# First attention of a four-layer network: norming two of eight batches ahead and six inside its loop, weighing a unit later, turning output rows in the sums' bank, first key copy on ACT

## The chip, the cores and the metric

One core of a Trainium2 chip runs the whole network in one launch. The metric is the time of that launch on the device, in microseconds; smaller is better. The engines are PE (matrix products; PEld is its loading of the stationary operand), DVE (vector), ACT (scalar functions), POOL and SP, whose queue issues most of the transfers. Each runs its own instructions in order and waits for the others on semaphores.

## The reference, cut to what matters

Four layers, each a norm, an attention and a feed-forward block that gates it. Only the first layer's norm and attention, and weights prepared for later layers, are touched. For x of 8 batches of 512 tokens with 128 features:

```python
x = L0_attn_x
xn = _layernorm(x, axis=-1)
s = _L0_attn_ref(xn, Wq, bq, Wk, bk, Wv, bv, Wo, bo)
g = _silu(_L0_ffn_ref(xn, ...))
x = x + s * g
...
def _layernorm(x, axis=-1, eps=1e-05):
    m = jnp.mean(x, axis=axis, keepdims=True)
    v = jnp.var(x, axis=axis, keepdims=True)
    return (x - m) / jnp.sqrt(v + eps)
...
# _sliding_window_attn: 16 heads of 8, blocks of 64 queries, each over its own and the previous block of keys
scores = jnp.einsum('bhnqd,bhnkd->bhnqk', qb, kw) * scale
valid = (t <= s_ + W) & (t >= s_ + 1) & (n * W - W + t >= 0)
scores = jnp.where(valid, scores, NEG)
attn = jax.nn.softmax(scores, axis=-1)
out = jnp.einsum('bhnqk,bhnkd->bhnqd', attn, vw)
out = out.transpose(...).reshape(B, S, D)
return out @ Wo.T + bo
```

## The kernel before

Tokens stand in the free dimension (x and xn are 128 features by 4096 tokens), in eight batches of 512. `network` loads x in eight pieces, loads constants of later layers, norms all eight batches (`layer_norm`), decodes the feed-forward block's weights (`l0_decode`), fills constants of layers 3 and 2 (`l2.fill`, `l1.fill`), runs `l0_attention`, then `l0_ffn`, and prepares scalars of the fourth layer (`l3_scalars`).

A framework places the semaphores and the buffers: a tile is written when the earlier tile in its buffer has been read by all its readers. What is issued through `in_order` keeps the written order on its engine; what isn't (`l0_decode`, `l3_scalars`, POOL's fills) is moved to where the framework finds room. So in the trace `l3_scalars` and the mixing weights of `l1.fill` run between 30 and 42 us, ahead of the attention's first scores.

`layer_norm` works on 512 tokens at a time: `centre` multiplies by a centring matrix into a PSUM bank (ps_c, tokens now in partitions), `spread` squares on ACT, sums on DVE (var) and takes the power -1/2 on POOL (rstd), `scale` multiplies on DVE (row), `turn` transposes back on PE (ps_t), `keep` copies to xn on ACT.

`l0_attention` first projects batch 0 (`project`: keys ps_k, copied four times under four head masks to kb, by DVE for c = 0 and 2 and by ACT for c = 1 and 3; queries ps_q; values ps_v in two parts of 4 and 3 windows). Then it runs a loop over 64 units, eight for each batch. Unit u is 128 queries and 8 heads:

- `scores(u)`: four products into a two-bank tile sc, DVE scales and masks it to e (the first DVE group called e), DVE takes the maximum mx, POOL subtracts it
- the exponential on ACT
- `turned(u)`: eight transposes on PE to two banks tp, ACT copies to pt
- `weigh(u)`: 64 by 9 products of pt with the values and a column of ones, into the bank of sums (av)
- after each pair of units, `norm`: DVE's reciprocal rec and product o; `out_rows`: PE turns o (tpo), ACT adds a bias into ot
- after each batch, `finish`: the output projection ps_o, which DVE scales to s

In iteration u each engine gets, in this order: turn of unit u, norm of the pair that ended with u-1 (u even), scores of u+3, output rows of that pair, exponential of u+2, weighing of u, `finish` of the batch before at the second unit of a batch, one step of the next batch's projection (ps_k in the first unit, the other two key copies in the second, ps_q, ps_v, ps_v). From unit 33 on a step of the feed-forward block's low-rank weights (`l0_low_rank`) comes once in eight units.

PSUM has eight banks: four for sc, three (pool p_t) for tp, tpo, ps_k, ps_q, ps_v and ps_o in turn, and one for av:

```python
sums = p_av.tile([P, 2, H, HD + 1], F32, tag="av", name="av")
...
tp = p_t.tile([P, 4, P], F32, tag="t", name="tpo")
pe.transpose(tp[:, 0, :], o.rearrange("p h d -> p (h d)"), net.ident)
```

All instructions issued through `in_order` carry one line, 84, in the profile; groups are told apart by the names of their tiles.

Of the kernel before, what the change touches and what calls it, by code (L numbers as in the profile page):

```python
# [9 lines left out]
F32 = mybir.dt.float32  # L10
I32 = mybir.dt.int32
AF = mybir.ActivationFunctionType
ALU = mybir.AluOpType
# [4 lines left out]
B = 8  # L18
# [9 lines left out]
class Net:  # L28
# [120 lines left out]

    def layer_norm(self, x, xn, gamma=None, beta=None, banks=(5, 3), free=False):  # L150

# [6 lines left out]
        with tc.tile_pool(name="ln_s", bufs=3) as sp, tc.tile_pool(  # L158
# [40 lines left out]

            for t in range(NTB + 3):  # L200
                if t < NTB:
                    centre(t)
                    spread(t)
                if 2 <= t < NTB + 2:
                    scale(t - 2)
                if t >= 3:
                    turn(t - 3)
                    keep(t - 3)
# [48 lines left out]

def l0_attention(net, xn, s_out, p0, w, bias):

# [5 lines left out]
    with ExitStack() as st:  # L265
# [22 lines left out]

        sums = p_av.tile([P, 2, H, HD + 1], F32, tag="av", name="av")

# [5 lines left out]
        def project(b):  # L296
# [5 lines left out]
            kb[b] = p2.tile([P, 4, S], F32, tag="kb", name="kb")  # L302
            for c in range(4):
                hm, hb = net.hm4[:, c : c + 1], kbias[:, c : c + 1]
                if c % 2:
                    act.activation(kb[b][:, c, :], ps, AF.Identity, scale=hm, bias=hb)
                    yield
                else:
                    dve.tensor_scalar(kb[b][:, c, :], ps, hm, hb, ALU.mult, ALU.add)
            ps = p_t.tile([P, S], F32, tag="t", name="ps_q")  # L310
            pe.matmul(ps, lhsT=w[:, 0, :], rhs=xb, start=True, stop=True)
# [46 lines left out]
        def turned(u):  # L358

            pts = []  # L360
            for g in range(2):
                tp = p_t.tile([P, 4, P], F32, tag="t", name="tp")
                for j in range(4):
                    pe.transpose(tp[:, j, :], e[u][:, 4 * g + j, :], net.ident)
                pt = p3.tile([P, 4, P], F32, tag="pt", name="pt")
                act.copy(pt, tp)
                pts.append(pt)
            return pts
# [25 lines left out]
        def out_rows(u, o):  # L394
            b, m = u // U, u // 2 % 4
            tp = p_t.tile([P, 4, P], F32, tag="t", name="tpo")
            pe.transpose(tp[:, 0, :], o.rearrange("p h d -> p (h d)"), net.ident)
            if m == 0:
                ot[b] = p2.tile([P, S], F32, tag="ot", name="ot")

            act.activation(ot[b][:, ts(m, P)], tp[:, 0, :], AF.Identity, bias=bias[:, 2:3])

# [10 lines left out]
        act.activation(e[0], e[0], AF.Exp)  # L413
        act.activation(e[1], e[1], AF.Exp)
        todo = iter(())
        for u in range(N + 2):
            if u < N and u % U == 0 and u // U + 1 < B:
                todo = project(u // U + 1)
            ended = u >= 1 and u <= N and u % 2 == 0
            if u < N:  # L420
                pts = turned(u)
            if ended:
                o = norm(u - 1)
            if u + AHEAD < N:
                scores(u + AHEAD)
            if ended:
                out_rows(u - 1, o)
            if u + 2 < N:
                act.activation(e[u + 2], e[u + 2], AF.Exp)
            if u < N:  # L430
                weigh(u, pts)
            if u >= U and u % U == 1:
                finish(u // U - 1)
            next(todo, None)
            if u == 4 * U:
                low = net.prep.l0_low_rank(
                    p0, lambda name: p_t.tile([P, S], F32, tag="t", name=name), pe, dve, act
                )
            if u > 4 * U and u % U == 6:
                next(low, None)  # L440


# [289 lines left out]
class L1Consts:  # L732
    E = 8

    def __init__(self, net, st):
        nc, tc, E = net.nc, net.tc, self.E
        self.net = net
        self.p1 = p1 = st.enter_context(tc.tile_pool(name="a1_c", bufs=1))
        self.rw = net.load(p1, "m1_r")
# [6 lines left out]
    def fill(self):  # L746
        net, nc, p1, E = self.net, self.net.nc, self.p1, self.E
        act = net.in_order(nc.scalar)
        self.w13 = net.load(p1, "m1_w13", act)
        self.w2 = net.load(p1, "m1_w2", act)  # L750

        w, par = self.w, self.par
        self.td = td = p1.tile([P, 1], F32, tag="td", name="td")
        act.activation(td, par[:, 0:1], AF.Exp)
        act.activation(td, td, AF.Copy, scale=-1.0)
        self.tf = par[:, 1:2]
        self.wm = wm = p1.tile([P, 3, 2, P], F32, tag="wm", name="wm")
        self.rest = rest = p1.tile([P, 3], F32, tag="rest", name="rest")
        act.activation(rest, par[:, 2:5], AF.Identity, scale=-1.0, bias=net.ones[:, 0:1])
        for i in range(3):  # L760
            act.activation(wm[:, i, 0, :], w[:, i, :], AF.Copy, scale=par[:, 2 + i : 3 + i])
            act.activation(wm[:, i, 1, :], w[:, i, :], AF.Copy, scale=rest[:, i : i + 1])
        act.activation(w[:, 3, :], w[:, 3, :], AF.Copy, scale=0.5)

# [20 lines left out]
        nc.gpsimd.memset(self.keep, 1.0)  # L785
        nc.gpsimd.memset(self.keep[:, :, 0:1], 0.0)


# [553 lines left out]
class L2Consts:  # L1342
# [4 lines left out]
    def __init__(self, net, st):  # L1347
# [4 lines left out]
        self.net = net  # L1352
        self.p1 = p1 = st.enter_context(tc.tile_pool(name="a2_c", bufs=1))
        self.w = net.load(p1, "a2_w")
# [1441 lines left out]
class Prepared:  # L2796
# [28 lines left out]

    def l0_decode(self):
        nc, wt, qw, sc = self.net.nc, self.f0_wt, self.qw, self.sc
        nc.vector.tensor_copy(wt, qw)
        nc.vector.tensor_scalar(wt, wt, 1.0 / 7.5, -1.0, ALU.mult, ALU.add)
        nc.vector.tensor_tensor(wt, wt, sc, ALU.mult)  # L2830

# [32 lines left out]

    def l3_scalars(self):

# [7 lines left out]
        raw = par[:, 1:5, :]  # L2874
        nc.vector.scalar_tensor_tensor(sp, raw, -1.0, raw, ALU.mult, ALU.min)
        nc.scalar.activation(sp, sp, AF.Exp)
        nc.scalar.activation(sp, sp, AF.Ln, bias=net.ones[:, 0:1])
        nc.vector.scalar_tensor_tensor(sp, raw, 0.0, sp, ALU.max, ALU.add)
        sig2, eta2, gam2, nu = (sp[:, i, :] for i in range(4))

        def vec(tag):
            return p1.tile([P, H], F32, tag=tag, name=tag)

        mu, nmu, v_e2, v_0, coef = vec("mu"), vec("nmu"), vec("v_e2"), vec("v_0"), vec("coef")
        nc.scalar.activation(mu, par[:, 0, :], AF.Exp, scale=-1.0)
        nc.vector.tensor_scalar(mu, mu, 1.0, None, ALU.add)
        nc.vector.reciprocal(mu, mu)
        nc.vector.tensor_scalar(mu, mu, 1e-4, None, ALU.add)
        nc.vector.tensor_scalar(nmu, mu, -1.0, None, ALU.mult)

        nc.vector.tensor_scalar(v_e2, nmu, 2.0, None, ALU.mult)
        nc.vector.reciprocal(v_e2, v_e2)
        nc.vector.tensor_tensor(v_e2, v_e2, sig2, ALU.mult)
        nc.vector.tensor_tensor(v_0, eta2, gam2, ALU.add)
        nc.vector.tensor_tensor(v_0, v_0, v_e2, ALU.subtract)
        nc.vector.tensor_scalar(coef, nu, float(DH), -0.5, ALU.add, ALU.mult)
        nc.vector.tensor_tensor(coef, coef, par[:, 5, :], ALU.mult)


        norm_0 = vec("norm_0")  # L2900
        nc.vector.tensor_tensor(norm_0[0:64], nu[0:64], v_e2[0:64], ALU.mult)
        nc.vector.tensor_tensor(norm_0[64:128], nu[64:128], v_0[64:128], ALU.mult)
        cs, ncs, inv_cs, g_v = vec("cs"), vec("ncs"), vec("inv_cs"), vec("g_v")


        nc.vector.scalar_tensor_tensor(cs, coef, -1.0, coef, ALU.mult, ALU.max)
        nc.vector.tensor_scalar(cs, cs, 1e-18, 2e-18, ALU.is_lt, ALU.mult)
        nc.vector.tensor_tensor(cs, cs, coef, ALU.add)
        nc.vector.tensor_scalar(ncs, cs, -1.0, None, ALU.mult)
        nc.vector.reciprocal(inv_cs, cs)  # L2910
        nc.vector.tensor_scalar(g_v, coef, -1.0, -0.5 * DH, ALU.mult, ALU.add)
        nc.vector.tensor_tensor(g_v, g_v, inv_cs, ALU.mult)
        self.scalars = nu, nmu, v_e2, v_0, norm_0, ncs, inv_cs, g_v


def network(tc, ins, out):
    with ExitStack() as ctx:
# [12 lines left out]
        with tc.tile_pool(name="prep_0", bufs=1) as p0:  # L2930
            w0, b0 = net.load(p0, "a0_w"), net.load(p0, "a0_b")
            prep.l0_load(p0)
            net.layer_norm(x, xn)
            prep.l0_decode()
            l2.fill()
            l1.fill()
            l0_attention(net, xn, s, p0, w0, b0)
            l0_ffn(net, x, xn, s, l1)
        prep.l3_scalars()
        l1_layer(net, x, xn, s, l1, l2)  # L2940
# [84 lines left out]
```

## Time and profile before

| what | us |
|---|---|
| median of 9 runs (lowest to highest) | 2330.58 (2326.09 to 2338.16) |
| the profiled execution | 2335.12 |
| its span | 2333.4 |
| busy over the span: PE, DVE, ACT, POOL | 2187.9, 2004.1, 1848.4, 1573.2 |
| busy from 100 to 150: PE, DVE, ACT, POOL | 47.81, 35.63, 33.16, 22.90 |
| first norm's first and last copy to xn | 13.40 and 29.11 |
| first scores of the attention | 42.44 |
| first turn tp (unit 0) | 50.12 |
| first product of the feed-forward block | 324.30 |

Durations of single instructions in the loop, by the rows of the trace from 100 to 315 us: e 1.22 and mx 1.22 on DVE, the subtraction 1.90 on POOL, the exponential 1.06 and a pt copy 0.59 on ACT, ot 0.37, rec 0.25, o 0.29, a key copy 0.81 on DVE and 0.78 on ACT. A view of the timeline has start, duration, engine, line, operation, output and inputs with shapes, the count, and in brackets how long the engine was idle before it and who released it. PE's listed durations overlap, since its matmuls are pipelined; the distance between starts is the cost of one.

### The profile page before, as it was taken

How to read it: one execution, taken by the hardware profiler on the slowest of the kernel's cores; microseconds unless marked ns; L12 is line 12 of the kernel's file. 1: busy time of each engine (PE TensorE's matmuls, PEld its weight loads, DVE VectorE, ACT ScalarE, POOL GpSimd, SP SyncE). 2: the span in 40 equal slices, each digit the busy share in tenths (PEclk: the TensorE clock that was granted, in tenths of full speed). 3: DMA queues.
4: the chain of work that ended last, by engine and by line, in shares of the span. 5: the costliest groups of instructions: out<-in, count | busy, mean ns of one | idle time of the engine just before them, and what ended most of it. 6: DMA issues, size and time to landing. Idle time of an engine off the chain costs nothing.

```text
span 2333.4 us, 48928 instructions
## 1 busy us (share of the span) xinstructions
PE 2187.9 (94%) x17762; PEld 1529.4 (66%) x17762; DVE 2004.1 (86%) x3595; ACT 1848.4 (79%) x3882; POOL 1573.2 (67%) x1410
## 2 busy tenths in 40 slices
PE   6999997999987999868999999999999999999998
PEld 4666675746633666645777777777777776777796
DVE  4677769786686999759999999999999999999885
ACT  4566656555543899838999999999999999999974
POOL 5344445264275788757788888888888888888644
PEclk7799989899997999979999999999999999999998
DMA  4000000012210000234443444444444444333200
GB/s 144 2 2 2 2 1 19 19 51 70 48 49 19 3 17 16 66 91 107 106 106 94 106 110 105 105 102 105 108 101 103 111 105 104 100 98 101 54 1 37
DMA packets 91617, 156.94 MB, mean 67 GB/s; under 512 B 20144, under 2 KB 44464, under 8 KB 91120
## 3 DMA queue, kind: packets, MB, share of 16 engines
q1 hardware_dynamic: 86736, 140.95, 23.1%
q0 software_dynamic: 4352, 8.92, 1.5%
q10 hardware_dynamic: 288, 3.93, 0.4%
q8 instruction: 142, 2.33, 0.4%
q14 instruction: 99, 0.81, 0.1%
HBM read 30.52 MB, written 12.06 MB: 18 GB/s over the span
## 4 chain that ended last, share of the span: by engine, by line
PE 58%; DVE 28%; POOL 5%; issue 3%; ACT 3%; DMA 2%; SPq 1%; DVEq 0%; ACTq 0%; POOLq 0%
PE sc L84 11%; DVE sc L84 7%; PE ps_av L84 6%; DVE r L84 6%; DVE y L84 6%; PE tp L84 5%; PE ps_u L84 5%; PE ps_kq L84 5%; PE av L84 3%; PE ps_n L84 3%; PE ps_ab L84 3%; PE ps_v L84 2%; DVE mx L84 2%; DVE e L84 2%; PE ps_y L84 1%
## 5 line engine op out<-in xcount | busy, mean ns | idle before, releaser
L84 POOL TENSOR_TENSOR ek<-E,kn 128x512 f32<-128x512 f32 (+3 forms) x512 | 434.1, 870 | 203.1 <-DMA kn<-nr 189.5
L84 POOL TENSOR_TENSOR e<-e,mx 128x1024 f32<-128x1024 f32 x112 | 212.1, 1900 | 190.3 <-DVE mx L84 93.5
L84 PE MATMUL sc<-r 128*128 128x512 f32 (+3 forms) x1024 | 306.6, 442 | 25.9 <-DVE y L84 18.9
L84 POOL TENSOR_TENSOR r<-r,rs 128x1024 f32<-128x1024 f32 x128 | 304.0, 2375 | 21.4 <-DMA rs<-r 18.6
L84 PE MATMUL ps_av<-u,at 128*128 128x128 f32 x2560 | 306.8, 275 | 0.3 <-DVE at L84 0.3
L84 PEld LDWEIGHTS ps_av<-u,at 128*128 128x128 f32 x2560 | 296.1, 192 | 1.5 <-ACT at L84 0.8
L84 ACT ACTIVATE y<-y,mn 128x384 f32<-128x384 f32 (+3 forms) x512 | 288.8, 570 | 4.0 <-DVE mn L84 3.2
L84 PEld LDWEIGHTS sc<-r 128*128 128x128 f32 x1024 | 164.1, 190 | 188.7 <-issue 115.4
L84 DVE CUSTOM_DVE_ANT_0 y<-y,ps_g,ncs 128x256 f32<-128x256 f32 (+3 forms) x512 | 254.0, 542 | 0.8 <-ACT y L84 0.8
L84 DVE SCALAR_TENSOR_TENSOR y<-sc,qn,V 128x512 f32<-128x512 f32 (+3 forms) x512 | 246.8, 544 | 8.6
L84 ACT ACT_TABLE_LOAD x179 | 229.7, 1283 | 6.1 <-DVE ex L84 2.1
L84 PEld LDWEIGHTS tp<-ident,y 128*128 128x128 f32 x1280 | 160.4, 140 | 112.1 <-issue 48.0
L84 PE MATMUL tp<-ident,y 128*128 128x128 f32 x1280 | 201.8, 273 | 2.6 <-ACT o L84 2.0
L84 DVE TENSOR_TENSOR sc<-sc,EF 128x1280 f32<-128x1280 f32 x128 | 191.9, 1499 | 4.3
L84 ACT COPY at<-tp 128x512 f32<-128x512 f32 x376 | 191.3, 509 | 5.2 <-PE tp L84 1.5
L84 DVE SCALAR_TENSOR_TENSOR sc<-sc,ek 128x1280 f32<-128x1280 f32 x128 | 189.9, 1483 | 2.9 <-POOL ek L84 1.4
L84 ACT ACTIVATE y<-y 128x1280 f32<-128x1280 f32 x128 | 163.4, 1277 | 6.0 <-DVE y L84 5.3
L84 DVE TENSOR_TENSOR r<-sn,ps_kq 128x1024 f32<-128x1024 f32 x128 | 155.4, 1214 | 12.1 <-ACT sq L84 12.1
L84 ACT ACTIVATE sq<-ps_kq 128x1024 f32<-128x1024 f32 x128 | 131.7, 1029 | 34.0 <-PE ps_kq L84 34.0
L84 DVE TENSOR_TENSOR r<-ct,ps_kq 128x1024 f32<-128x1024 f32 x128 | 155.4, 1214 | 0.0
L84 POOL TENSOR_TENSOR s<-s,o 128x512 f32<-128x512 f32 x116 | 148.4, 1279 | 2.5 <-ACT o L84 2.4
L84 ACT ACTIVATE e<-e 128x1024 f32<-128x1024 f32 x112 | 117.3, 1061 | 40.4 <-POOL e L84 39.9
(462 smaller groups left out, 5042.1 us busy)
## 6 DMA issues: line engine op xcount, KB each, us to landing
rs<-r SPq DMA_DIRECT2D x256, 256.0 KB, 3.8
kn<-nr SPq DMA_DIRECT2D x512, 64.0 KB, 2.0
yrows<-yy SPq DMA_DIRECT2D x36, 128.0 KB, 1.8
ct<-trig SPq DMA_DIRECT2D x16, 256.0 KB
EF<-E SPq DMA_DIRECT2D x16, 256.0 KB, 2.7
EF<-E SPq DMA_DIRECT2D x16, 192.0 KB
m_w<-m_w ACTq DMA_DIRECT2D x1, 2560.0 KB, 9.3
x<-x SPq DMA_DIRECT2D x8, 256.0 KB, 3.7
```

What stands on the lines that cost most here:

```text
L84: ins = op(*args, **kwargs)
```

## The change

- `layer_norm` takes a count and norms two batches ahead. The other six are normed inside the attention's loop: centring (four products on PE, a copy to SBUF on ACT), square (ACT), sums (DVE) and root (POOL), scaling (four ACT instructions in place of one on DVE), turn and copy, each at a given unit.
- `weigh` of a unit is issued one iteration later, so the pair's norm and output rows come at odd units and `finish` at the third unit of a batch. pt has four buffers instead of three.
- The output rows are turned into the free columns of the bank that holds the sums (av), not into a bank of p_t.
- ACT makes the first key copy (c = 1), then DVE (c = 0), then ACT, then DVE.
- Loads of later layers' constants come behind the first layer's loads on SP's queue; the two large expert weights go from ACT's queue to SP's. `l0_decode` (its last product on POOL instead of DVE), the mixing weights of `l1.fill` and `l3_scalars` become steps that are issued in order in the loop, three to a batch from unit 9 on.

```diff
-    def layer_norm(self, x, xn, gamma=None, beta=None, banks=(5, 3), free=False):
+    def layer_norm(self, x, xn, gamma=None, beta=None, banks=(5, 3), free=False, n=NTB):
...
-            for t in range(NTB + 3):
-                if t < NTB:
+            for t in range(n + 3):
+                if t < n:
...
-        sums = p_av.tile([P, 2, H, HD + 1], F32, tag="av", name="av")
+        both = p_av.tile([P, TB], F32, tag="av", name="av")
+        n_av = 2 * H * (HD + 1)
+        sums = both[:, 0:n_av].rearrange("p (m h d) -> p m h d", m=2, h=H)
+        tpo = both[:, n_av : n_av + P]
...
-            for c in range(4):
+            for c in (1, 0, 3, 2):
                 hm, hb = net.hm4[:, c : c + 1], kbias[:, c : c + 1]
                 if c % 2:
                     act.activation(kb[b][:, c, :], ps, AF.Identity, scale=hm, bias=hb)
-                    yield
                 else:
                     dve.tensor_scalar(kb[b][:, c, :], ps, hm, hb, ALU.mult, ALU.add)
+                    yield
...
-                pt = p3.tile([P, 4, P], F32, tag="pt", name="pt")
+                pt = p5.tile([P, 4, P], F32, tag="pt", name="pt")
...
-            tp = p_t.tile([P, 4, P], F32, tag="t", name="tpo")
-            pe.transpose(tp[:, 0, :], o.rearrange("p h d -> p (h d)"), net.ident)
+            pe.transpose(tpo, o.rearrange("p h d -> p (h d)"), net.ident)
...
-            act.activation(ot[b][:, ts(m, P)], tp[:, 0, :], AF.Identity, bias=bias[:, 2:3])
+            act.activation(ot[b][:, ts(m, P)], tpo, AF.Identity, bias=bias[:, 2:3])
...
+        def centre(b):
+            ps = p_t.tile([P, 4, P], F32, tag="t", name="ps_c")
+            for k in range(4):
+                pe.matmul(
+                    ps[:, k, :], lhsT=x[:, ts(4 * b + k, P)], rhs=net.cmat,
+                    start=True, stop=True,
+                )
+            mid[b] = p2.tile([P, 4, P], F32, tag="lc", name="lc")
+            act.copy(mid[b], ps)
+
+        def square(b):
+            sqs[b] = p2.tile([P, 4, P], F32, tag="sq", name="sq")
+            act.activation(sqs[b], mid[b], AF.Square, scale=net.inv_root)
+
+        def spread(b):
...
+            dve.tensor_reduce(var, sqs.pop(b), AX.X, ALU.add)
+            dve.tensor_scalar(var, var, EPS, None, ALU.add)
+            pool.tensor_tensor(std[b], var, net.neg_half.to_broadcast([P, 4]), ALU.pow)
+
+        def scale_rows(b):
+            for k in range(4):
+                act.activation(
+                    mid[b][:, k, :], mid[b][:, k, :], AF.Copy, scale=std[b][:, k : k + 1]
+                )
+
+        def turn_rows(b):
+            ps = p_t.tile([P, 4, P], F32, tag="t", name="ps_t")
+            for k in range(4):
+                pe.transpose(ps[:, k, :], mid[b][:, k, :], net.ident)
+            act.copy(xn[:, ts(b, S)], ps.rearrange("p k q -> p (k q)"))
+
+        norms = {}
+        for b in range(2, B):
+            c = U * (b - 3) + 7 if b > 2 else 1
+            for part, at in (
+                (centre, c), (square, c + 1), (spread, c + 2), (scale_rows, c + 4),
+                (turn_rows, U * (b - 2) + 6),
+            ):
+                norms.setdefault(at, []).append((part, b))
+
+        def early():
+            yield from net.prep.l0_decode(dve, pool)
+            yield from l1.mixing(act)
+            yield from net.prep.l3_scalars(dve, act)
+
+        rest = early()
         todo = iter(())
-        for u in range(N + 2):
+        pts = {}
+        for u in range(N + 3):
             if u < N and u % U == 0 and u // U + 1 < B:
                 todo = project(u // U + 1)
-            ended = u >= 1 and u <= N and u % 2 == 0
+            ended = u >= 3 and u % 2 == 1
             if u < N:
-                pts = turned(u)
+                pts[u] = turned(u)
             if ended:
-                o = norm(u - 1)
+                o = norm(u - 2)
             if u + AHEAD < N:
                 scores(u + AHEAD)
             if ended:
-                out_rows(u - 1, o)
+                out_rows(u - 2, o)
             if u + 2 < N:
                 act.activation(e[u + 2], e[u + 2], AF.Exp)
-            if u < N:
-                weigh(u, pts)
-            if u >= U and u % U == 1:
+            if 1 <= u <= N:
+                weigh(u - 1, pts.pop(u - 1))
+            if u >= U and u % U == 2:
                 finish(u // U - 1)
             next(todo, None)
+            for part, b in norms.get(u, ()):
+                part(b)
+            if u >= U and u % U in (1, 3, 6):
+                next(rest, None)
...
-            if u > 4 * U and u % U == 6:
+            if u > 4 * U and u % U == 5:
                 next(low, None)
...
     def fill(self):
...
-        self.w13 = net.load(p1, "m1_w13", act)
-        self.w2 = net.load(p1, "m1_w2", act)
+        self.w13 = net.load(p1, "m1_w13")
+        self.w2 = net.load(p1, "m1_w2")
...
+    def mixing(self, act):
...
+        for i in range(3):
+            act.activation(wm[:, i, 0, :], w[:, i, :], AF.Copy, scale=par[:, 2 + i : 3 + i])
+            act.activation(wm[:, i, 1, :], w[:, i, :], AF.Copy, scale=rest[:, i : i + 1])
+            yield
...
-        nc.vector.tensor_tensor(wt, wt, sc, ALU.mult)
+        pool.tensor_tensor(wt, wt, sc, ALU.mult)
+        yield
...
+        dve.scalar_tensor_tensor(sp, raw, -1.0, raw, ALU.mult, ALU.min)
+        act.activation(sp, sp, AF.Exp)
+        act.activation(mu, par[:, 0, :], AF.Exp, scale=-1.0)
+        yield
+        act.activation(sp, sp, AF.Ln, bias=net.ones[:, 0:1])
+        yield
...
             prep.l0_load(p0)
-            net.layer_norm(x, xn)
-            prep.l0_decode()
+            l2.load()
+            l1.load()
+            net.layer_norm(x, xn, n=2)
             l2.fill()
             l1.fill()
-            l0_attention(net, xn, s, p0, w0, b0)
+            l0_attention(net, x, xn, s, p0, w0, b0, l1)
             l0_ffn(net, x, xn, s, l1)
-        prep.l3_scalars()
```

## The prediction

> **What bounds the kernel now.** I read the busy time by stretch first, then the timeline of the head (0 to 62 us), then TensorE's own timeline through the loop, then the rows of single tiles. The change touches only what runs before 324 us, where the first feed-forward block begins; nothing behind it is edited, and the scalars for the fourth layer that move into the loop are needed only much later.
>
> The stretches (busy time of each engine, then granted clock, DMA share, GB/s):
>
> ```profile
> 0.00:20.00 20.00, 11.45 (x59) 11.10 (x60) 7.58 (x17) 6.04 (x9) 13.84 (x59) 0.91 0.70 212
> 20.00:60.00 40.00, 26.82 (x144) 17.22 (x146) 21.44 (x47) 18.82 (x36) 15.82 (x19) 0.63 0.27 104
> 60.00:100.00 40.00, 39.52 (x414) 25.54 (x406) 22.89 (x26) 20.34 (x32) 14.48 (x8) 0.73 0.01 2
> 100.00:150.00 50.00, 47.81 (x636) 31.20 (x628) 35.63 (x42) 33.16 (x54) 22.90 (x13) 1.00 0.01 2
> ```
>
> From 100 us on PE is busy 47.8 of 50, DVE 35.6, ACT 33.2, POOL 22.9: the loop is PE's. Before 60 us no engine is full: that is a chain. And the clock is 0.63 and 0.73 of full until about 82 us, with PE busy all the while.
>
> The head, from the timeline (start, duration, then what):
>
> ```profile
> 10.88 4.00 POOL L84 TENSOR_TENSOR rstd<-var,neg_half 128x4 f32<-128x4 f32 x4
> 11.96 0.69 DVE L84 TENSOR_TENSOR row<-ps_c,rstd 128x512 f32<-128x512 f32 x1 [0.82 <-POOL rstd L84]
> 13.40 0.59 ACT L84 COPY xn<-ps_t 128x512 f32<-128x512 f32 x1 [2.00 <-PE ps_t L84]
> ...
> 29.75 2.07 PE L84 MATMUL ps_k<-xn,a_w 128*128 128x512 f32 x2 [0.68 <-ACT xn L84]
> 36.19 0.76 ACT L84 ACTIVATE kb<-ps_k,kbias,hm 128x512 f32<-128x512 f32 x1
> 36.97 1.28 ACT L2877 ACT_TABLE_LOAD   x1
> 40.05 0.76 ACT L84 ACTIVATE kb<-ps_k,kbias,hm 128x512 f32<-128x512 f32 x1
> 40.86 1.65 PE L84 MATMUL ps_v<-a_w,xn 128*128 128x128 f32 x6 [6.18 <-ACT kb L84]
> 42.44 1.95 PE L84 MATMUL sc<-kb,q 32*64 32x512 f32 x16
> ```
>
> Eight batches are normed until 29.7; then ACT makes its first key copy at 36.2 and its second at 40.05, with the other layers' preparation ahead of them, and the first scores start at 42.44.
>
> The loop at full clock:
>
> ```profile
> 128.03 0.30 PE L84 MATMUL tpo<-ident,o 128*128 128x128 f32 x1 [0.24 <-DVE o L84]
> 128.26 1.11 PE L84 MATMUL av<-vw,pt 128*64 128x9 f32 x32
> 128.37 0.37 ACT L84 ACTIVATE ot<-tpo,a_b 128x128 f32<-128x128 f32 x1 [0.47 <-PE tpo L84]
> 130.46 0.81 DVE L84 TENSOR_SCALAR kb<-ps_k,hm,kbias 128x512 f32<-128x512 f32 x1
> 131.30 0.78 ACT L84 ACTIVATE kb<-ps_k,kbias,hm 128x512 f32<-128x512 f32 x1 [0.76 <-DVE kb L84]
> 132.61 1.13 PE L84 MATMUL av<-vw,pt 128*64 128x9 f32 x32 [0.30 <-ACT pt L84]
> 134.63 0.60 PE L84 MATMUL tp<-ident,e 128*128 128x128 f32 x4
> 135.71 0.66 PE L84 MATMUL tp<-ident,e 128*128 128x128 f32 x4 [0.48 <-DVE s L84]
> ```
>
> One batch of eight units (first turn of one batch, 130.25, to that of the next, 162.10) takes 31.85 us. PE's holes in it: 0.31 twice where the output rows' turn waits for DVE's o (the last sc ends at 127.72, tpo starts at 128.03), 0.37 where av waits for pt, 0.57 where the second tp waits for a bank that DVE's s still reads, 0.14 behind one more tpo: 1.7 in all. The work itself is 30.1.
>
> **The change, part by part.** The sum is made against the profiled execution, 2335.1 us (its span is 2333.4, and 1.7 lie around it); the median shown is 2330.6.
>
> Head. Two batches are normed instead of eight. POOL's root still comes at 10.88 (it is behind the same fills); the second root ends at 12.9, its rows are scaled (0.69), turned (0.7 to 0.8) and copied (0.59), so ps_k can start at about 15.1 instead of 29.75: 14.6 saved. The attention's weights, issued at 12.2 us on SP's queue now, go right behind x there (4.5 us), so they aren't late. Then the chain without the strangers: ps_k 2.07, four key copies one after the other (0.2 to start, 0.78 and 0.81 alternating), the second ps_v (1.55), then scores: 7.0 us against 12.7 (29.75 to 42.44). Saved: 5.7. Head **-20.3** (from -18, if the fills or masks are later, to -24, if POOL's roots come when var is ready at 7.9). The two large expert weights go from ACT's queue to SP's: the timeline has 1.10 us for these two issues on ACT, inside the 5.7; on SP they stand behind everything needed early.
>
> Norms woven in. Per batch PE gets eight instructions of ps_c (0.128 each as ps_v, 8 in 1.00) and four turns (0.51): 1.54, for six batches **+9.2**. ACT gets a copy 0.59, square 0.60, four row scalings of about 0.3 (the 128x128 copies at 34.2 have that step), a copy 0.59: 3.0 per batch, onto 21.7 of 31.85. DVE gets 0.9, POOL one root of 1.0. All three stay under PE, so they are costed at nothing, except that behind the last turn (unit 7 of 8) ACT comes to the output rows late by about 0.25: +1.5.
>
> Weighing a unit later takes the 0.37 pt wait away; turns and centring between units give DVE time for o, which takes the 0.31s away; no tpo in the three banks takes the 0.57 and the 0.14 mostly away. Removed: 1.7 in each of six warm batches, some 2 in the others: **-12.3**. Given back: the turn of unit 3 finds its second bank held by s or q for about 0.3, seven times: +2.1.
>
> Output rows in the sums' bank. This is the dearest edit. Two engines never read one bank together in this trace: 14 times ACT's key copy waits for DVE's key copy of the same ps_k, though neither needs the other's data (131.30 above, straight after 130.46+0.81):
>
> ```profile
>   DVE kb L84: 26.3, 14
> ```
>
> So I take it that PE's av, which now writes the bank that ACT's ot reads, waits for ot too. In the rows above av starts 0.23 behind tpo; ot ends at 128.74, and PE's starts follow ACT's ends by 0.06 (322.38 to 322.44), so av would start at 128.80: 0.54 later. Thirty-two such units: **+17.3**. Nothing else is on PE's queue ahead of the stalled av that could fill it; scores, turns and projections stand behind. Lower bound 0 (if regions of a bank are told apart), upper 0.9 (ACT one ot late).
>
> [...]
>
> First key copy by ACT. DVE's first copy now waits for ACT's. ps_k ends, 0.2, ACT 0.78, DVE 0.72 to its successor, and the successor is now rec of an ended unit (odd units end now): rec 0.28, o 0.29, 0.12 to tpo: 2.42 after ps_k, where PE, with tp 0.97 and sc 1.02, is there at 1.99. 0.44, seven times: **+3.1** (0 to 5).
>
> Preparation moved into the loop: some 35 small DVE and ACT instructions of 0.1 to 0.55 us, and POOL's 128x768 product (1.4 by its 128x1024 row of 1.90), hidden under PE, whose cover is a unit's slack in pt. Ln's table and Exp's again (1.28 each) meet one unit: **+2** (0 to 4).
>
> Clock. In this execution it stayed at half from 50 to 81.8 us, which cost some 15; it fell for 3.4 us at 170.5 and 269.5, each behind the stretch with split tp, sc, tpo and av, and from 310 to 327. The batch behind the start now has centring beside the projections, so I expect it up a unit or two earlier: -6 (0 to -10). But holes of 0.5 to 1.0 beside sc and av make more such thin stretches: +6 (0 to +15). Net **0**.
>
> [...]
>
> Sum: -20.3 +9.2 +1.5 -12.3 +2.1 +17.3 +3.1 +2 +0 = +2.6: **2337.7**, said as 2338, which is 0.3% over the median of 2330.6. About 0.2% (4.7 us) is what can be told from no change.
>
> **The rivals.**
>
> The bank doesn't stall PE (faster). If av starts 0.23 behind tpo as now, 17.3 go: 2320. For it: the columns are disjoint, and a write beside a read of the same bank isn't shown in this trace. Against it: the 14 waits. It decides from a stall under 0.16 us, where the sum passes 2325.9.
>
> The clock gains (about no change). Everything as forecast, but the start is up 10 earlier and no new falls come: 2338-10 = 2328. For it: six centrings and turns are full-size matmuls. Against: the holes.
>
> The clock falls in most batches (slower). Two falls a batch of 3.4 us at half rate, plus one that lasts until the next projections, 15 us over the loop: 2353. For it: a hole of 0.98 in the first ended unit of a batch stands between sc and av, longer than the 0.57 behind which it fell twice. Against: it didn't fall behind the 0.31s.
>
> **How the numbers follow.** Forecast 0.45 (its own range 2327 to 2349); no bank stall 0.25; clock gains 0.12; clock falls 0.18. Low end: 2320 less 4 for a longer head gain, 2316. High end: 2353 and 3 more for ACT's lateness, 2356. Faster by over 0.2%: 0.25, half of 0.12, and 0.03 of the forecast, 0.34. Slower: 0.18 and 0.30 of the forecast, 0.48. Within: 0.18.
>
> **What would show it.** First scores near 22 us, not 42. Per ended unit: av starts right behind ot's end (0.06), not 0.23 behind tpo. A warm batch of 34.5 us, not 31.85. DVE's key copy waits for ACT's, and tpo behind it waits for o. The feed-forward block starts near 327, not 324. Wrong: av not waiting for ot; a head that gains under 15; a clock at half much longer or shorter than 30 us.

## The result, and the profile after

The changed kernel takes 2385.91 us (median of 15 runs, 2362.69 to 2396.98) beside 2329.24 (46 runs of the kernel before): **ratio 1.0243, 95% interval 1.0227 to 1.026**. It is 2.4% slower; 2338 was forecast, and 2356 was the range's upper end. The profiled execution took 2381.53 us, with a span of 2379.8.

The stretches of the changed kernel (columns as before: stretch, length, busy time of PE, PEld, DVE, ACT, POOL, granted clock, DMA share, GB/s):

```profile
0.00:20.00 20.00, 10.17 (x36) 7.25 (x36) 4.79 (x10) 5.11 (x8) 15.33 (x67) 0.83 0.68 194
20.00:60.00 40.00, 33.48 (x346) 20.43 (x347) 27.73 (x28) 24.56 (x40) 18.07 (x10) 0.82 0.30 113
60.00:100.00 40.00, 38.14 (x345) 25.91 (x345) 21.21 (x27) 19.14 (x32) 12.78 (x7) 0.67 0.01 2
100.00:150.00 50.00, 47.39 (x523) 30.84 (x521) 30.91 (x36) 29.50 (x51) 21.71 (x12) 0.81 0.00 1
```

From 100 to 150 us the clock is 0.81 where it was 1.00, and PE does 523 products where it did 636, although it is busy for nearly as long (47.39 for 47.81). Busy time alone hides this.

The head, chosen rows from the timeline of the changed kernel (start, duration, what, and in brackets the idle time before and who ended it):

```profile
10.88 2.04 POOL L84 TENSOR_TENSOR rstd<-var,neg_half 128x4 f32<-128x4 f32 x2
...
14.86 0.59 ACT L84 COPY xn<-ps_t 128x512 f32<-128x512 f32 x1 [0.41 <-PE ps_t L84]
15.50 2.07 PE L84 MATMUL ps_k<-xn,a_w 128*128 128x512 f32 x2 [0.68 <-ACT xn L84]
17.66 0.78 ACT L84 ACTIVATE kb<-ps_k,kbias,hm 128x512 f32<-128x512 f32 x1 [2.22 <-PE ps_k L84]
18.47 0.81 DVE L84 TENSOR_SCALAR kb<-ps_k,hm,kbias 128x512 f32<-128x512 f32 x1 [3.31 <-ACT kb L84]
...
20.73 0.94 PE L84 MATMUL ps_v<-a_w,xn 128*128 128x128 f32 x6 [0.92 <-ACT q L84]
21.59 1.11 PE L84 MATMUL sc<-kb,q 32*64 32x512 f32 x16
```

The keys start at 15.50 (15.1 was forecast), the scores at 21.59 (forecast: near 22; before: 42.44). The first turn comes at 28.43, 21.7 us earlier than before. The head did what it should.

TensorE's timeline in the loop of the changed kernel, which answers to the rows at 128 us of the kernel before:

```profile
109.31 0.33 PE L84 MATMUL av<-ident,o 128*128 128x128 f32 x1
110.10 1.11 PE L84 MATMUL av<-vw,pt 128*64 128x9 f32 x32 [0.46 <-ACT ot L84]
...
117.08 1.09 PE L84 MATMUL sc<-kb,q 32*64 32x512 f32 x8
118.48 0.33 PE L84 MATMUL av<-ident,o 128*128 128x128 f32 x1 [0.32 <-DVE o L84]
119.26 1.11 PE L84 MATMUL av<-vw,pt 128*64 128x9 f32 x32 [0.46 <-ACT ot L84]
120.30 1.52 PE L84 MATMUL tp<-ident,e 128*128 128x128 f32 x8
121.75 1.98 PE L84 MATMUL sc<-kb,q 32*64 32x512 f32 x8
123.66 1.88 PE L84 MATMUL av<-vw,pt 128*64 128x9 f32 x32
```

The turn of the output rows (now named av<-ident,o, since it lies in that tile) is followed by the weighing 0.79 us later, not 0.23: the forecast hole. Of the 0.79 the turn itself fills 0.33, so the rows show 0.46 as idle; the hole costs 0.56 against the order before. At 118.48 stands the other one, 0.32 in wait for DVE's o behind the key copy. Then the same eight scores that took 1.09 take 1.98, with no wait ahead of them. The stretches around that moment:

```profile
111.00:120.00 9.00, 8.23 (x109) 5.43 (x105) 6.18 (x8) 6.74 (x11) 5.15 (x3) 1.00 0.01 2
120.00:123.00 3.00, 3.00 (x30) 1.70 (x26) 2.94 (x4) 2.20 (x7) 1.90 (x1) 0.64 0.02 5
123.00:132.00 9.00, 9.00 (x56) 4.77 (x52) 3.65 (x5) 2.90 (x4) 2.90 (x2) 0.55 0.00 0
132.00:134.00 2.00, 1.54 (x38) 1.24 (x34) 1.66 (x2) 1.31 (x2) 0.00 (x0) 1.00 0.00 0
```

The clock falls to half, and PE is busy 9.00 of 9.00 until it is up again. DVE's maximum (1.22, at 125.13) and ACT's exponential (1.06, at 122.98) beside it take as long as before. This repeats some eighteen times in the loop; before, it happened three times behind the start.

**Where 46.4 us of span came from.** From the first turn to the first product of the feed-forward block the loop took 341.8 us, before 274.2: +67.6, less 21.7 of the head. The time at half clock in it, summed from the trace's clock record, is 160.8 us, before 52.3. In the rows above PE's products at half clock take 1.8 and 1.7 times as long (1.98 for 1.09, 1.88 for 1.11); at half of its time lost, this is worth some (160.8 - 52.3)/2 = 54 us, an estimate (49 if a us at half clock costs 0.45, as bank_only below suggests). PE's idle time grew from 11.2 to 20.8. What is left, loop less idle less half of the half-clock time, is 240.6 beside 236.8. The rest of the program, from the feed-forward block on, takes 2009.6 beside 2009.1.

### The profile page after: what moved, and what is told of

Its sections match the earlier page's. It is cut to its first block, busy times and chain, and to the rows that moved or that the text cites. A ratio compares the mean times of both kernels' runs of the same rounds, so it can differ in the third digit from the quotient of the medians.

```text
span 2379.8 us, 48883 instructions
## 1 busy us (share of the span) xinstructions
PE 2235.7 (94%) x17762; PEld 1559.0 (66%) x17762; DVE 2009.7 (84%) x3588; ACT 1861.5 (78%) x3912; POOL 1574.1 (66%) x1411
## 4 chain that ended last, share of the span: by engine, by line
PE 58%; DVE 24%; POOL 6%; ACT 4%; issue 3%; DMA 2%; SPq 2%; POOLq 0%; ACTq 0%; DVEq 0%
PE sc L84 11%; DVE sc L84 7%; PE tp L84 6%; DVE y L84 5%; DVE r L84 5%; PE ps_av L84 5%; PE ps_kq L84 4%; PE av L84 4%; PE ps_u L84 4%; PE ps_ab L84 3%; PE ps_n L84 2%; PE ps_v L84 2%; PE ps_o L84 2%; POOL ek L84 2%; SPq L2205 1%
## 5 line engine op out<-in xcount | busy, mean ns | idle before, releaser
L84 PE MATMUL sc<-r 128*128 128x512 f32 (+3 forms) x1024 | 311.6, 448 | 26.4 <-DVE y L84 23.4
L84 DVE SCALAR_TENSOR_TENSOR e<-sc,maskFalse 128x1024 f32<-128x1024 f32 (+1 forms) x96 | 90.4, 952 | 89.5 <-PE sc L84 84.0
```

The costliest lines, as they stand in the source:

```text
L84: ins = op(*args, **kwargs)
```

## The experiments

Theory H: PE's short holes (0.3 to 0.55 us), which the new wait makes between thin products, bring the clock down, and the clock makes nearly all of the loss. The first rival: the shared bank itself costs it. The second: it comes from weaving norms and preparation in. Medians of the kernel before differ by 1% from chip to chip (2329.90, 2351.28, 2349.26 and 2357.05 beside these runs), so kernels are compared by their ratio to it on the same chip; two ratios from different chips are less sure than their intervals say. The table's last four columns are of one profiled execution each, in us: the loop as above, half clock in it, PE idle in it, and loop less idle less half of the half clock.

| kernel | ratio to before (95%) | loop | half clock | idle | rest |
|---|---|---|---|---|---|
| before | 1 | 274.2 | 52.3 | 11.2 | 236.8 |
| changed | 1.0243 (1.0227 to 1.026) | 341.8 | 160.8 | 20.8 | 240.6 |
| own_bank | 0.9971 (0.9941 to 1.0) | 285.2 | 70.2 | 7.9 | 242.2 |
| turn_after | 0.9943 (0.9912 to 0.9974) | 273.8 | 48.5 | 10.4 | 239.2 |
| bank_only | 1.0408 (1.0337 to 1.0479) | 359.2 | 212.4 | 23.6 | 229.4 |
| filled | 1.0314 (1.0242 to 1.0386) | 346.8 | 118.1 | 31.5 | 256.3 |
| hole_apart | 1.0352 (1.0295 to 1.0409) | 338.2 | 157.3 | 24.8 | 234.8 |
| hole_worked | 0.9977 (0.995 to 1.0005) | 290.3 | 41.2 | 9.7 | 260.0 |
| late_keys | 0.9984 (0.9964 to 1.0005) | 291.8 | 94.0 | 7.2 | 237.6 |
| weave_only | 1.0175 (1.013 to 1.022) | 331.3 | 136.9 | 22.0 | 240.9 |
| spread_out | 0.9895 (0.9868 to 0.9923) | 267.4 | 32.0 | 11.7 | 239.7 |
| half_holes | 1.0038 (1.0007 to 1.0069) | 298.9 | 80.6 | 15.5 | 243.1 |
| own_keys | 1.0101 (1.0062 to 1.0139) | 321.3 | 140.5 | 11.6 | 239.5 |
| spread_own | 0.9939 (0.992 to 0.9959) | 287.8 | 72.7 | 10.1 | 241.3 |

The last column stays within 229 and 243 but where work was added (filled, hole_worked): the kernels differ by half clock, and by holes. bank_only does the work of the kernel before and has 229.4 for 236.8, so half a us lost per us at half clock is somewhat too much; 0.45 would make the two equal.

The clock of the other executions is on record too, as a mean over the whole launch. The traces' clock records of the kernel before and the changed one have full and half clock alone, so twice the missing share of it is the time at half clock, by medians (lowest to highest): changed 276 us (212 to 316), own_bank 173 (159 to 202), turn_after 170 (130 to 216), hole_worked 130 (92 to 149), half_holes 196 (169 to 257), hole_apart 298 (273 to 329), bank_only 344 (311 to 372); the kernel before has 154 to 179 by the chip. So these readings don't hang on one execution.

**own_bank** undoes one edit of the changed kernel.

```diff
-            pe.transpose(tpo, o.rearrange("p h d -> p (h d)"), net.ident)
+            tp = p_t.tile([P, 4, P], F32, tag="t", name="tpo")
+            pe.transpose(tp[:, 0, :], o.rearrange("p h d -> p (h d)"), net.ident)
...
-            act.activation(ot[b][:, ts(m, P)], tpo, AF.Identity, bias=bias[:, 2:3])
+            act.activation(ot[b][:, ts(m, P)], tp[:, 0, :], AF.Identity, bias=bias[:, 2:3])
```

> The changed kernel with the output rows turned in a bank of p_t again, as before; all else as changed. Theory H (the 0.55 us holes behind each tpo cost themselves, 32 x 0.55 = 17.6, and what they do to the clock: 161.7 us at half clock in the changed loop against 52.3 before, so some 55 us of work lost): both go, 2315 to 2345 us, less than 90 us at half clock. Rival W (the woven norms and the key order thin the loop out, the holes only cost themselves): about 2386 - 17.6 = 2368, half clock still over 120 us.

Measured: 0.9971, half clock 70.2. The one edit, in the changed kernel, makes a difference of 2.7%; without it, the kernel that weaves norms and preparation in isn't slower than before. The second rival is out as the cause of this loss, but weaving isn't harmless by itself: with DVE making the first key copy (own_keys and weave_only, below) the woven kernel is slower than before without the sums' bank, too.

**turn_after** keeps the sums' bank and lets nothing wait behind the turn: in odd units PE weighs first, then turns.

```diff
-            if ended:
-                out_rows(u - 2, o)
             if 1 <= u <= N:
                 weigh(u - 1, pts.pop(u - 1))
+            if ended:
+                out_rows(u - 2, o)
```

> The changed kernel with the turn in the sums' bank kept, but issued behind the unit's weighing instead of ahead of it, so that no av stands behind a tpo. H: no hole, so 2310 to 2345 us and less than 90 us at half clock; it may beat the kernel before, since the head's 21 us stay. W: 2368, half clock over 120 us. If the wait were only moved (the next tp or av waiting for ot), about 2386.

Measured: 0.9943, half clock 48.5. TensorE's timeline of turn_after:

```profile
98.72 1.09 PE L84 MATMUL sc<-kb,q 32*64 32x512 f32 x8
100.12 1.10 PE L84 MATMUL av<-vw,pt 128*64 128x9 f32 x32 [0.31 <-DVE o L84]
101.16 0.33 PE L84 MATMUL av<-ident,o 128*128 128x128 f32 x1
101.32 1.04 PE L84 MATMUL tp<-ident,e 128*128 128x128 f32 x8
...
107.11 0.66 PE L84 MATMUL tp<-ident,e 128*128 128x128 f32 x4 [0.34 <-ACT q L84]
```

The wait for ot is gone, as the next turn of scores follows 0.16 behind; the bank is shared as in the changed kernel.

**bank_only** puts the sums' bank alone into the kernel before (the hunks on `both`, `tpo` and ot of the diff).

> The kernel before with this one edit alone: the output rows are turned in the sums' bank. H: 32 holes of 0.55 us and more time at half clock, 2350 to 2385 us, half clock over 90 us against 52. W: the holes only, 2329 + 17.6 = 2347 at most, half clock near 52.

Measured: 1.0408, half clock 212.4: slower, as H has it, but well beyond the 2350 to 2385 (1.009 to 1.024) that it expected. The edit alone loses more than the whole change does. The kernel before has no centring and no turns of norms between its units, which may be why; that wasn't tried by itself.

**hole_apart** makes the hole without the shared bank: in the kernel before, a one-column product that reads ot stands behind the turn, so that PE waits for ot.

```diff
             act.activation(ot[b][:, ts(m, P)], tp[:, 0, :], AF.Identity, bias=bias[:, 2:3])
+            pe.matmul(
+                tp[0:1, 1, 0:1], lhsT=net.ones[:, 0:1], rhs=ot[b][:, m * P : m * P + 1],
+                start=True, stop=True,
+            )
```

> The kernel before, the output rows still turned in a bank of p_t; behind each tpo PE also makes one product of a single column of ot, which nothing reads, so that av stands behind ACT's ot here too, without a shared bank. If an idle hole of some 0.6 us per pair is what counts: 32 x 0.65 = 21 us and a clock that falls as in the kernel with the bank alone, 55 to 110 us over before, over 120 us at half clock. If it is the shared bank itself: 21 us over before at most, half clock near 52.

TensorE's timeline of hole_apart:

```profile
126.72 0.30 PE L84 MATMUL tpo<-ident,o 128*128 128x128 f32 x1 [0.24 <-DVE o L84]
127.48 0.19 PE L84 MATMUL tpo<-ot,ones 128*1 128x1 f32 x2 [0.46 <-ACT ot L84]
127.60 1.11 PE L84 MATMUL av<-vw,pt 128*64 128x9 f32 x32
```

Measured: 1.0352, its interval overlapping that of bank_only. The same 0.46 of wait, no shared bank, the same loss within their intervals: the hole costs it, not the bank.

**filled** and **hole_worked** both put four repeated transposes of the odd unit (of no use, 0.5 us of PE) near the hole of the changed kernel; filled ahead of the turn, hole_worked behind it, in the hole.

```diff
+        def again(u):
+            if u in held:
+                pt, tp = held.pop(u)
+                for j in range(4):
+                    pe.transpose(tp[:, j, :], e[u][:, 4 + j, :], net.ident)
+                act.copy(pt, tp)
```

> The changed kernel, with the second four transposes of each odd unit issued a second time between its scores and its tpo (the same output again): 32 x 0.51 = 16.4 us of work more for PE, no hole removed. H with the clock: PE works in the middle of the thin stretch, the clock falls less, 2340 to 2375 us in spite of the added work. W, or holes that cost only themselves: 2386 + 16.4 = 2402.

> The changed kernel with the hole kept and filled: behind the tpo of each odd unit, where PE waits for ot, its second four transposes are issued a second time (the same output again), 0.51 us in a hole of 0.55. No time of PE is won by it in itself. If the clock answers to the idle stretch: half clock under 90 us instead of 161.7, 35 to 55 us under the changed kernel, 0 to 1% over before. If the loss is in the waiting for the bank and not in the clock: as the changed kernel, 2.4% over before.

filled missed: 1.0314, which is the 2402 of the rival W. By its terms it isn't W's case: half clock fell to 118.1 from 160.8, while idle time grew to 31.5 from 20.8 and the added work is 15.7. It isn't a fair trial of H either: pt's copy, held back behind the repeated transposes, stood ahead of ot on ACT, so the hole grew, as its timeline shows (0.83 of wait):

```profile
125.52 0.27 PE L84 MATMUL av<-ident,o 128*128 128x128 f32 x1
126.63 1.11 PE L84 MATMUL av<-vw,pt 128*64 128x9 f32 x32 [0.83 <-ACT ot L84]
```

hole_worked mended that, and its timeline has no idle time behind the turn:

```profile
99.99 0.33 PE L84 MATMUL av<-ident,o 128*128 128x128 f32 x1
100.16 0.60 PE L84 MATMUL tp<-ident,e 128*128 128x128 f32 x4
100.78 1.10 PE L84 MATMUL av<-vw,pt 128*64 128x9 f32 x32
```

With 32 x 0.5 = 16 us of useless work more than the changed kernel it is 2.6% faster than it (0.9977 for 1.0243), and its half clock is 41.2 for 160.8. From the turn to av it is 0.79, as in the changed kernel, but PE is at work in between. The time is slightly better than the 0 to 1% over before that was expected.

**half_holes** has the sums' bank for every second pair.

```diff
+            tp = tpo if m % 2 else p_t.tile([P, 4, P], F32, tag="t", name="tpo")[:, 0, :]
+            pe.transpose(tp, o.rearrange("p h d -> p (h d)"), net.ident)
```

> The changed kernel with every second pair's output rows turned in a bank of p_t and the others' in the sums' bank, so 16 holes of 0.55 us in place of 32. Holes theory: half of the 17.6 us of stall goes (about 9), and the clock falls less often: half clock from first turn to feed-forward 90 to 135 us, between the 70.2 of own_bank and the 161.7 of the changed kernel, and the ratio to before 1.003 to 1.018. Rival (the clock needs two holes in a window of about 3.4 us to fall, or is locked to the batch as a whole): as own_bank, ratio 0.995 to 1.001, or as the changed kernel, 1.022 to 1.026.

Measured: 1.0038, in H's range at its lower end, with 80.6 at half clock (90 to 135 expected) in an execution of 2350 where the median is 2362. Half the holes cost a quarter of what all of them do (1.0038 from own_bank's 0.9971, all of them 1.0243): the clock's share grows faster than the holes, though its executions spread from 2350 to 2388 and the three ratios come from different chips.

**weave_only** undoes three edits: the sums' bank, weighing later and ACT's first key copy. **late_keys** is turn_after, and **own_keys** is own_bank, with DVE making the first key copy:

```diff
-            for c in (1, 0, 3, 2):
+            for c in range(4):
...
                     act.activation(kb[b][:, c, :], ps, AF.Identity, scale=hm, bias=hb)
+                    yield
                 else:
                     dve.tensor_scalar(kb[b][:, c, :], ps, hm, hb, ALU.mult, ALU.add)
-                    yield
```

> The change without three of its edits: the turn in a bank of p_t, the weighing in its own unit and DVE's key copy first, so only the norms and the preparation moved. Head -21, norms' work +9, holes of the old loop (1.7 us a batch) kept but for those that the woven work covers: 8 to 14 us under before, half clock 50 to 75 us. If the weaving itself makes the clock fall: above before.

> The changed kernel with the turn behind the weighing and with DVE making the first key copy, as before the change. The hole of 0.38 us ahead of the first pair's av, where DVE's o is late, goes seven times: 2.7 us less than with the turn behind the weighing alone, 0.6 to 0.8% under before. If ACT's copies then come late for the next turn (as 0.57 us once a batch before), no gain: 0.5% under before.

> The changed kernel with tpo in a bank of p_t and DVE making the first key copy, so that two of its edits are undone. Beside own_bank (ACT first): the hole behind ps_k of 0.32 to 0.40 where av or tpo waits for DVE's o goes, seven times, some 3 us, and one thin stretch less per batch: 2325 to 2340, 0.3 to 0.8% under the kernel before. Rival (late_keys went that way: no gain, as ACT's later key copy comes to hold the banks longer): same as own_bank, within 0.2% of it. Beside weave_only (+1.75%), from which it differs only by weighing a unit later: 40 us or more less.

All three missed their first forecast. weave_only was to be faster than before and is 1.75% slower, with 136.9 at half clock: the other case that its text names. late_keys was to gain 2.7 us over turn_after and gained none: 0.9984 for 0.9943. Its idle time did fall, 7.2 for 10.4, but half clock is 94.0 for 48.5, with one fall of 64.9 us from 259.5 on; why it lasts so long isn't shown. own_keys is 1.3% slower than own_bank by their ratios, from this edit alone. The timeline of all engines in own_keys shows the hole behind it:

```profile
109.66 1.22 DVE L84 TENSOR_REDUCE mx<-e 128x8 f32<-128x1024 f32 x1
...
110.80 0.80 DVE L84 TENSOR_SCALAR kb<-ps_k,hm,kbias 128x512 f32<-128x512 f32 x1
...
111.63 0.78 ACT L84 ACTIVATE kb<-ps_k,kbias,hm 128x512 f32<-128x512 f32 x1 [1.75 <-DVE kb L84]
...
112.83 1.06 ACT L84 COPY pt<-tp 128x512 f32<-128x512 f32 x2
...
113.46 0.33 PE L84 MATMUL tpo<-ident,o 128*128 128x128 f32 x1 [1.28 <-ACT pt L84]
```

With DVE first, ACT's copy waits 1.75 for DVE's, which stands behind a maximum; ACT's square of the woven norm and its pt copies stand behind that, and tpo needs a bank that they free: PE is idle for 1.28. With ACT first, the wait is on DVE, and PE's hole is 0.41 in own_bank:

```profile
103.67 0.81 DVE L84 TENSOR_SCALAR kb<-ps_k,hm,kbias 128x512 f32<-128x512 f32 x1 [0.26 <-ACT kb L84]
...
105.11 0.30 PE L84 MATMUL tpo<-ident,o 128*128 128x128 f32 x1 [0.41 <-ACT pt L84]
```

So ACT's first key copy is worth 1.3% in the woven loop where tpo needs a bank of p_t, and 0.4% (late_keys beside turn_after, whose intervals overlap) where it doesn't. weave_only has a like hole (1.02, in front of av, for pt). From it own_keys differs only by weighing a unit later, and is 0.7% faster by the ratios (intervals 1.013 to 1.022 and 1.0062 to 1.0139): a small gain at most, since the intervals still meet, and not the 40 us that were expected. All three comparisons go across two chips.

**spread_out** takes the second hole of turn_after, at 107.11 above, where ps_q and ps_o hold two of the three banks: ps_o goes to the sixth unit.

```diff
-            if u >= U and u % U == 2:
+            if u == N + 2 or (u >= U and u % U == 5):
```

> As turn_after (output rows turned in the sums' bank, behind the unit's own weighing), with the batch's output projection ps_o moved from the third unit of a batch to the sixth (for the last batch it stays at the third unit behind it). In turn_after the third and fourth unit have the second turn waiting 0.34 to 0.43 us for a bank of p_t, seven times. Holes theory: without them about 3 us of wait go and fewer falls of the clock come (half clock from first turn to feed-forward under 45 us, from 51.8), 2313 to 2330, 0.7 to 1.1% under the kernel before. Rival (these holes were not what brought the clock down): the wait returns at the sixth unit, where centring's copies use the same three banks, and the time is that of turn_after, 0.57% under the kernel before.

Measured: 0.9895, within H's 0.7 to 1.1%, and half clock 32.0. But idle time didn't fall by 3 us: it is 11.7 for 10.4. The waits of tp for ACT's q (2.1 us in turn_after) are gone, and those of av for DVE's o have grown from 6.9 to 8.7. So what is gained is in the clock, with the projection's products standing in other units. From 60 to 150 us the clock is at full:

```profile
60.00:100.00 40.00, 38.66 (x525) 26.36 (x521) 31.47 (x39) 29.23 (x51) 22.71 (x13) 1.00 0.01 2
100.00:150.00 50.00, 49.19 (x677) 33.99 (x681) 39.87 (x47) 38.78 (x75) 25.60 (x16) 1.00 0.01 2
```

PE does 677 products from 100 to 150, before 636 and the changed kernel 523.

**spread_own** is spread_out with tpo in a bank of p_t again (the diff of own_bank).

> As spread_out, with the output rows turned in a bank of p_t again, so that of the edits on holes only the sums' bank is undone. It tells what the sums' bank is worth once no product waits behind it. If the sums' bank helps (tpo and its copy no longer stand in the rotation of three banks): spread_out is 0.3 to 0.8% faster than this one, whose ratio to before would be 0.993 to 0.998, with a hole of 0.3 to 0.5 us per pair in the first ended unit of a batch and half clock over 40 us. Rival (the bank's place never mattered, only where the turn stands): the same time as spread_out, ratio 0.987 to 0.992.

Measured: 0.9939, so spread_out is 0.44% faster, on two chips and with intervals that just meet (up to 0.9923, from 0.992). The sums' bank seems to help a little, once no product waits behind the turn.

spread_out beats both kernels: 1.05% faster than before, and by the two ratios 3.4% faster than the changed kernel (0.9895/1.0243).

## Why the prediction was wrong

The mechanism of the stall was right; the step that failed is the term of the clock: "But holes of 0.5 to 1.0 beside sc and av make more such thin stretches: +6 (0 to +15). Net **0**." It measured some +50 (49 to 54, the estimate above). Its first half was right in kind: from the first turn on, the start is at half clock for 7.1 us, before 31.6, which is worth -12 for the -6 forecast. The second half, put at +6 without a count of how many thin stretches there would be, came to about +60 to +66: 153.7 us at half clock behind the start for 20.7.

- **Head, -20.3:** the first scores come 20.9 earlier, the first turn 21.7. Right.
- **Output rows in the sums' bank, +17.3 (0.54 each):** 0.79 for 0.23, so 0.56 each, in the rows above; over the 31 turns with an av behind them, from turn to av, 26.4 us for 8.7, which is +17.6. Right, and the rival that PE doesn't stall is gone. The waits of the changed kernel from 28 to 370 us (time, count, longest) show them, and DVE's key copy waiting for ACT's, which is the order the edit made:

```profile
PE av L84 <- ACT ot L84: 15.0, 30, 1.4
...
DVE kb L84 <- ACT kb L84: 1.8, 7, 0.3
```

- **The place of the data:** hole_apart (1.0352, with a wait and no shared bank) and turn_after (0.9943, with a shared bank and no wait behind the turn) show that the loss goes with the wait.
- **First key copy by ACT, +3.1 (0.44 each):** its hole is 0.32 a batch, near what was said. But the term compared it with the old order as it ran in the old loop. In the woven loop the old order costs a hole of 1.28 (own_keys), so the edit gains 1.3% there. The sign was wrong, and "DVE's first copy now waits for ACT's" was only half of the question: who waited before is to be asked too.
- **Woven norms, lateness, preparation, holes removed:** not measured one by one. All terms of the loop but the clock's summed to 9.2+1.5-12.3+2.1+17.3+3.1+2 = +22.9; measured are 67.6-54.3 = +13.3, with the estimate of half a us lost per us at half clock. Without the clock the kernel would have been faster than before by about 8 us (3 at 0.45 per us), not slower by 2.6. One part of the preparation can be read: where Ln's and Exp's tables are loaded, at 246.7 and 249.6, av waits 1.40 for ot, not 0.46.
- **The rival "the clock falls in most batches"** was the case that came. It had the right mechanism and half of the place ("between sc and av"), and its price was 15 us where some 50 came, for two reasons: it put two falls of 3.4 us in a batch, while in the changed kernel ten of eighteen last 10.2 or 17.1 us; and its argument against, "it didn't fall behind the 0.31s", took single holes one by one, without what PE does in the 3.4 us around them (last section). The batch itself then drags: ps_k starts at 115.15 and 163.09, 47.9 us for the 34.5 forecast.

What to look for had been written down: "a clock at half much longer or shorter than 30 us". It was 160.8 us.

## What to carry to other kernels

Before an edit puts a wait on PE, look at the granted clock around it and count what full-size work stands beside the wait: this loop lost several times the wait itself (some 50 us, an estimate, for 17.6 of waits). Put the product that has to wait behind one that needn't (turn_after, 0.9943 for 1.0243), and try spreading large products (projections) over units that lack them (spread_out, 0.9895). When two engines take turns on one bank, as ACT and DVE do here with ps_k, let the engine with the shorter queue behind it be the one that waits (PE's hole 0.41 in own_bank for 1.28 in own_keys), and price the order that is left as well as the new one.

## What the runs showed of the hardware that was not expected

**The clock changes at steps of 3.413 us, and its falls follow steps with little full-size work.** In the clock records of the kernel before and the changed one every stretch in the loop lasts 3.413 us or a whole multiple of it (6.827, 10.240, 17.067). The slices of 0.25 us of all fourteen traces agree: every fall and rise in the loop stands a whole number of 3.413 us from the others of the same execution, within 0.005 us.

For the kernel before and the changed one I cut the loop at these steps (every one that touches it) and summed in each the time of PE's full-size products: all but the scores (sc, 32 rows) and the weighing (av<-vw,pt, 9 columns), each from its start to the next one's, at most to its end. The bounds of the rows are chosen afterwards, on these two executions. Steps at full clock:

| full-size work, us | before: steps, followed by half clock | changed: steps, followed by half clock |
|---|---|---|
| under 0.95 | 1, 1 | 17, 16 |
| 0.95 to 1.1 | 14, 1 | 6, 2 |
| over 1.1 | 50, 1 | 30, 0 |

Steps at half clock:

| full-size work, us | before: steps, followed by full clock | changed: steps, followed by full clock |
|---|---|---|
| under 2.0 | 10, 0 | 26, 1 |
| 2.0 to 2.8 | 4, 1 | 9, 4 |
| over 2.8 | 3, 3 | 14, 14 |

PE's busy time alone doesn't part them. Of the steps at full clock with 2.9 to 3.0 us of it, none of 6 in the kernel before was followed by half clock, and 11 of 16 in the changed one. Of the steps at half clock with over 3.38 us of it, 33 of 56 were followed by half clock again.

This goes some way to explain the size. Eight of the eighteen falls of the changed kernel follow steps with 0.90 us of full-size work. Each of these eight holds the whole string of scores, turn, hole and av; the one from 178.85 to 182.26 is shown here (a ninth such step, from 100.34, with 0.91, wasn't followed by a fall):

```profile
179.04 1.09 PE L84 MATMUL sc<-kb,q 32*64 32x512 f32 x8
180.06 0.33 PE L84 MATMUL av<-ident,o 128*128 128x128 f32 x1
180.85 1.10 PE L84 MATMUL av<-vw,pt 128*64 128x9 f32 x32 [0.46 <-ACT ot L84]
181.88 1.77 PE L84 MATMUL ps_v<-a_w,xn 128*128 128x128 f32 x8
```

The string takes 1.02+0.79+1.03 = 2.84 and leaves 0.57 for other products; with the turn's own 0.33 that is 0.90. By the same sum, an estimate, av 0.23 behind the turn gives 1.13+0.23 = 1.36, and with the old 0.31 ahead of tpo 1.05: in the first table one step of 80 over 1.1 was followed by a fall, and 3 of 20 from 0.95 to 1.1. The three falls of the kernel before, behind its start, follow 0.91, 0.97 and 1.32 (the last a step without scores). At half clock the same products fill nearly twice the time (1.98 for 1.09), and all seventeen steps over 2.8 hold a projection, centring, a low-rank product or the feed-forward block's first ones. Between them the clock mostly stayed down: many falls last three or five steps.

So the length of a hole alone says little. In own_keys, by slices of 0.25 us, PE is idle for 1.28 from 148.6 us, in the step from 146.6, and the clock stays up; it is idle for 1.29 from 181.8, in the step from 180.8, and the clock falls at 184.2. In the first step no slice has over 8 products; in the second three in a row, behind the hole, have 11 to 15. Over the loop own_keys is idle for 11.6 us and at half clock for 140.5; spread_out is idle for 11.7 and at half clock for 32.0.

Nor does a busy PE bring the clock up by itself: from 123 to 132 us of the changed kernel it was busy 9.00 of 9.00 at 0.55.

What the clock answers to isn't known from this: the tables are a count over two executions, and the rows from 0.95 to 1.1 and from 2.0 to 2.8 go both ways.
